# Reordering the start of layers 1 and 2: where the first products stand among the scores, and which transfers go ahead of the first spare rows

## The chip, the cores and the metric

The kernel runs on one core of a Trainium2 chip. Its engines are TensorE (PE, matrix products; the profile shows its weight loads apart as PEld), VectorE (DVE), ScalarE (ACT), GpSimd (POOL) and SyncE (SP), whose queue issues nearly all DMAs. Each engine works off its own list of instructions in order; semaphores hold an instruction back until its inputs are there. The metric is the device time of one execution in microseconds.

## The reference

The whole program is a convolution block followed by an attention block, on 32 images of 1024 channels and 14x14 positions. Only the first block matters here. It is made of three "lookup" layers: each splits its input channels into codebooks, scores every position against 16 centroids of each codebook, takes the softmax over the 16, and multiplies the result with a table of outputs:

```python
def _amm(patches, centroids, lut, inv_temp):
    B, D, H, W = patches.shape
    ncb, k, sub = centroids.shape
    v = patches.reshape(B, ncb, sub, H * W).transpose(0, 3, 1, 2)
    scores = 2.0 * einsum('blcs,cks->blck', v, centroids) - sum(centroids**2, -1)[None, None]
    attn = softmax(scores * inv_temp, axis=-1)
    out = einsum('blck,cko->blo', attn, lut)
    return out.transpose(0, 2, 1).reshape(B, -1, H, W)

out = _amm(x, c1_centroids, c1_lut, c1_invt)                       # layer 1: 1024 -> 256 channels
out = relu(_bn(out, bn1_g, bn1_b))
out = _amm(_extract3x3(out, 1), c2_centroids, c2_lut, c2_invt)     # layer 2: 3x3 patches of 256 -> 256
out = relu(_bn(out, bn2_g, bn2_b))
out = _amm(out, c3_centroids, c3_lut, c3_invt)                     # layer 3: 256 -> 1024
```

`x` here is the group-normalised input, and `_bn` takes its statistics over the whole batch, so a layer has to end before the next one can start.

## The kernel before, in words

Layers 1 and 2 are both run by one function, `units`. A unit is one pair of images (392 positions) times one eighth of the codebooks; there are 16 pairs, so 128 units in each layer, and unit `u` belongs to pair `u // 8` and table `u % 8`. A unit goes through these stations:

- `score(u)`: 4 score tiles by PE into PSUM (a pool `scores` of four buffers), then four exponentials by ACT (L576) into a tile `t`, one of six that are used in turn.
- `token_major`: a 32x32 block transpose on DVE (L588), and from unit 2 on a first halving addition on POOL (L591).
- `softmax`: sum, reciprocal and transpose back on DVE (L607, L609, L619), then POOL multiplies `t` by the reciprocals (L626). A unit with `u % 4 == 0` gives its first quarter to a tile `spare` (L621); for unit 0 POOL does the rest in three steps.
- `spare_rows` (L725, L728): DMAs on SP's queue that put rows of `spare` into every sixteenth row of `t`. Those rows are free because the 16 softmax weights of a codebook add to one: the last is left out, and the tables are corrected for it. So the first quarter of one unit in four is spread over the other quarters of the four, and that unit has 12 matmul records in place of 16.
- `lut(u)`: the products of `t` with the unit's table (L748) into the accumulators `po`, 12 or 16 matmul records.

The order in which these are written is the order on every engine (`tc.manual_schedule`). In step `i`, `units` writes `score(i + 4)` and its exponentials, the transpose of unit `i + 3`, the softmax of unit `i + 2` (of unit `i + 3` for units 0 and 1), then `side(i)`, a list of work by step, and last the products of one unit. The loop starts at `i = -4`. A small table at L784 says which products stand in the first steps:

```python
k = {-2: 0, -1: 1, 0: -1, 1: -1}.get(i, i) if ahead > 2 else i
```

So product 0 stands in step -2, product 1 in step -1, none in steps 0 and 1, and from step 2 on product `i`.

The eight tables of a layer lie in `weights`. `packed_lut` gives for each table the pieces of its preparation: `own` (piece 1, the load from HBM, L689 for layer 1 and four DMAs at L692 for layer 2), `less` (piece 2, a correction: two matmuls with `less_last`, L700, each evicted by ACT, L701), `keep` (piece 3, a DMA to a DRAM tile `tables`, L704) and `others` (piece 4, a DMA back from it into another table, L707).

In layer 1 the side work of the first steps also holds the group normalisation of the second image pair: statistics and means (L264, L274, L282), a power on POOL (L295), and the scaling of `x` on ACT (L825).

Layer 2 needs 3x3 patches. `store_pair(p, h)` normalises one half (128 of the 256 channels) of a pair into one of two `pads` (ACT, L990) and writes it by three DMAs (225 KB each, L1002) to two DRAM tiles `h1d`. `load_patches(u)` reads the patches of a unit from there by six DMAs (L1012) into one of four buffers. Units with table 0 to 3 use half 0, tables 4 to 7 half 1. `score2(u)` also loads the patches of unit `u + 3`. Before the first step, layer 2 writes this on SP's queue: the stores of half 0 of the first pair, patches 0 and 1 (a third of them on ACT's queue), `keep` of table 0, patches 2, `others` of table 0, patches 3, the stores of half 1, `others` of tables 1 to 3, and `own` of table 7. `own` of tables 0 to 6 is written late in layer 1. `side2` has the corrections of tables 4 to 7 in steps -3 to 0 and the stores of the later pairs, at a step given by the dictionary at L1065.

Of the kernel before, what the change touches and what calls it, by code (L numbers as in the profile page):

```python
# [149 lines left out]
def conv_preact_kernel(ctx: ExitStack, tc: tile.TileContext, a: dict, out: bass.AP):  # L150
# [3 lines left out]
    NP = B // 2  # L154
# [352 lines left out]
    def layers(exact, early=None):  # L507
# [38 lines left out]
        def tap_row(dy, dx):  # L546
            return 8 * dx + dy if dx < 2 else 3 + dy
# [25 lines left out]
        def exponentials(t, scs, bias):  # L573

            for j, sc in enumerate(scs):
                nc.scalar.activation(  # L576
                    t[:, j, : sc.shape[1]],
                    sc,
                    AF.Identity if exact else AF.Exp,
                    bias=bias[:, j : j + 1],  # L580
                )

        def token_major(pool, t, two=False, halve=False):


            tf = t.rearrange("p j n -> p (j n)")
            tt = pool.tile([P, tf.shape[1]], F32, tag="tt", name="tt", bufs=2 if two else 1)
            nc.vector.transpose(tt, tf)  # L588
            tv = tt.rearrange("p (m k) -> p m k", k=KC)
            if halve and not exact:  # L590
                nc.gpsimd.tensor_tensor(tv[:, :, :8], tv[:, :, :8], tv[:, :, 8:], ALU.add)  # L591
                tv = tv[:, :, :8]
            return tt, tv
# [123 lines left out]
        def spare_rows(ts, u):  # L717


            q = u % 4  # L720
            t, kept = ts[u % len(ts)], spares[u // 4 % 2]
            if exact and q == 0:
                nc.sync.dma_start(kept, t[:, 0, :N2])
            if q:
                nc.sync.dma_start(t[15::16], kept[q - 1 :: 4])  # L725
                return
            for j in range(1, 4):
                nc.sync.dma_start(t[15::16, j, :], kept[4 * j - 1 :: 16])  # L728
# [3 lines left out]
        def units(ahead, ts, pool, luts, score, bias, dst, stats, side, last, halve=False):  # L732

            n = 8 * NP
            po, late, tts = [], [], {}

            def lut(u):
                p, b = divmod(u, 8)  # L740
                if b == 0:
                    po[:] = [
                        ps_po.tile([P, 512], F32, tag="po", name="po")[:, :N2] for h in range(2)
                    ]
                j0 = 0 if b % 4 else 1
                order = [(h, j) for h in range(2) for j in range(j0, 4)]
                for h, j in order if b == 7 else sorted(order, key=lambda k: k[1]):
                    nc.tensor.matmul(  # L748
                        po[h],
                        luts[b][:, j, h * P : (h + 1) * P],  # L750
                        ts[u % len(ts)][:, j, :N2],
                        start=(b == 0 and j == j0),
                        stop=(b == 7 and j == 3),
                    )
                if b == 7:
                    for h in range(2):
                        o = dst[:, h, p * N2 : (p + 1) * N2]
                        nc.scalar.copy(o, po[h])
                        late.append((stats[:, h, p, :], o))

            for i in range(-ahead, n):
                u = i + ahead
                if u < n:
                    scs = score(u)
                    exponentials(ts[u % len(ts)], scs, bias[:, 4 * (u % 8) :][:, :4])
                u = i + ahead - 1
                if 0 <= u < n:
                    tts[u] = token_major(pool, ts[u % len(ts)], halve, halve and u >= DIRECT)
                if halve and u >= DIRECT:
                    u = u - 1 if u > DIRECT else n  # L770
                if 0 <= u < n:
                    softmax(
                        pool,
                        u,
                        ts[u % len(ts)],
                        *tts.pop(u),
                        spare=spares[u // 4 % 2] if u % 4 == 0 else None,
                        steps=(1, 1, 1) if u == 0 and not exact else None,
                    )
                    spare_rows(ts, u)  # L780
                while late:
                    nc.vector.bn_stats(*late.pop(0))
                side(i)
                k = {-2: 0, -1: 1, 0: -1, 1: -1}.get(i, i) if ahead > 2 else i  # L784
                if k >= 0:
                    lut(k)
            for h in range(2):
                nc.vector.bn_stats(*late.pop(0))
                last(h)
# [4 lines left out]
        with ExitStack() as s:  # L794
# [43 lines left out]
            def side(i):  # L838
                for f in todo.pop(i, []):
                    f()  # L840
# [10 lines left out]
            luts2 = [packed_lut(2, b) for b in range(8)]  # L851
# [120 lines left out]
        with ExitStack() as s:  # L972
# [4 lines left out]
            NPB = 4  # L977
# [10 lines left out]
            def store_pair(p, h, engines=(nc.sync,)):  # L988
                t = pads[h]
                nc.scalar.activation(  # L990
                    t.rearrange("p (i r c) -> p i r c", r=15, c=15)[:, :, :14, :14],
                    out1[:, h, p * N2 : (p + 1) * N2].rearrange(
                        "p (i r c) -> p i r c", r=14, c=14
                    ),
                    AF.Relu,
                    bias=bi1[:, h : h + 1],
                    scale=sc1[:, h : h + 1],
                )
                for x in range(3):
                    c0 = LEAD + 2 * p * IMG + 1 - x  # L1000
                    v = h1d[x // 2][h, :, :, c0 : c0 + 2 * IMG]
                    engines[x % len(engines)].dma_start(v[:, x::2] if x < 2 else v, t)  # L1002
# [3 lines left out]
            def load_patches(u, engines=(nc.sync,)):  # L1006
                p, b = divmod(u, 8)
                h, g = divmod(b, 4)
                for n, (src, rows) in enumerate(zip(h1d, (8, 16))):
                    for dy in range(3):  # L1010
                        c0 = LEAD + 2 * p * IMG + 15 * (dy - 1)
                        engines[dy % len(engines)].dma_start(  # L1012
                            pbuf[u % NPB][tap_row(dy, 2 * n) :: rows, :, :SPAN],
                            src[h, 4 * g : 4 * g + 4, :, c0 : c0 + SPAN].rearrange(
                                "q r n -> r q n"
                            ),
                        )
# [10 lines left out]
            load_patches(2)  # L1028
            luts2[0][4]()
            load_patches(3)  # L1030
            store_pair(0, 1)
            for b in range(1, 4):
                luts2[b][4]()
            luts2[7][1]()
            w9, bias2 = parts[2]

            def score2(u):
                if 0 < u and u + NPB - 1 < 8 * NP:
                    load_patches(u + NPB - 1)
                scs = [scores(N2) for j in range(4)]  # L1040
                for c in range(4):
                    for j, sc in enumerate(scs):
                        r = slice(32 * j, 32 * j + 27)
                        v = pbuf[u % NPB][r, c].rearrange("p (i r c) -> p i r c", r=15, c=15)
                        nc.tensor.matmul(
                            sc[32 * c : 32 * c + 32],
                            w9[r, u % 8 * 4 + c],
                            v[:, :, :14, :14],
                            start=True,
                            stop=True,  # L1050
                        )
                return scs

            ahead = 1 if exact else 4

            def side2(i):

                for b in range(4, 8):
                    if i == max(b - 7, -ahead):
                        luts2[b][2]()  # L1060
                    if i == max(b - 4, 0):
                        luts2[b][4]()
                if i == max(-2, -ahead):
                    luts2[4][3]()
                p = {1: 1}.get(i + ahead, (i + ahead + 9) / 8)  # L1065
                if p in range(1, NP):
                    for h in range(2):
                        store_pair(int(p), h)
                if i == 60:
                    bias3, biases = score_biases(ps_tr, big, st, 3, raw[3], P, 2, mask8, 4)  # L1070
                    parts[3] = score_matrices(big, 3, "", raw[3], mask8), bias3
                    parts["biases3"] = biases
                if i == 64:
                    parts["biases3"]()
                next_lut3(i - 8 * (NP - 1) - 1)
# [1213 lines left out]
```

## Time and profile before

| | us |
|---|---|
| median of three runs | 3391.9 |
| lowest and highest of them | 3390.8, 3393.84 |
| the profiled execution's own time | 3393.07 |
| its span, first to last instruction | 3390.4 |
| PE busy | 3303.7 (97%) |
| DVE busy | 2871.6 (85%) |
| POOL busy | 2528.6 (75%) |
| ACT busy | 1790.1 (53%) |
| mean granted clock of TensorE | 0.994 |

Layer 1 runs from about 20 to 834 us of the span, layer 2 from there to about 1648 us, each with a start of some 50 us in which its pipeline fills.

How to read the profile's lines. A timeline line is: start, length, engine, line of the kernel, operation, output <- inputs, shapes, count of instructions that were merged into the line, and in brackets how long the engine was idle before it and what ended that idle time. PE's matmul records are halves: one fp32 matmul shows as two. A line of a table of stretches is: the stretch, its length, busy time and instruction count of PE, PEld, DVE, ACT and POOL, the granted clock (1.00 is full speed), the mean share of the DMA engines, and GB/s. "SPq" lines are the issue of DMAs by SP, not their transfer.

### The profile page before, as it was taken

The page shows a single profiled execution, that of the slowest core. Times are in us where ns is not written, and L with a number is a line of the kernel's source. Part 1 is how long each engine was busy: PE and PEld are TensorE (multiplying, and loading weights), DVE is VectorE, ACT ScalarE, POOL GpSimd, SP SyncE. Part 2 cuts the span into 40 slices and gives each one's busy share as a digit, 9 for nine tenths or more (in the row PEclk, how much of TensorE's full clock was granted, in tenths as well). Part 3 has the DMA queues.
Part 4 walks back from the last instruction along what each step waited for, and adds up shares of the span by engine and source line. Part 5 has one row for each costly group of instructions (what it writes and reads, how often), then busy time and mean ns, then how long its engine had stood idle before and what let it go on. Part 6 is the DMA issues. An engine that isn't in the chain of part 4 may idle for free. (4 is left out here: it accounts for less than half of the span.)

```text
span 3390.4 us, 61032 instructions
## 1 busy us (share of the span) xinstructions
PE 3303.7 (97%) x22287; PEld 2015.7 (59%) x22287; DVE 2871.6 (85%) x4174; ACT 1790.1 (53%) x4419; POOL 2528.6 (75%) x1562
## 2 busy tenths in 40 slices
PE   7999999999899999999999999999999999999998
PEld 4555555554344444454478888876666666666665
DVE  7999999997788898888666666655899999989996
ACT  4555555554444444444311111108888888888885
POOL 4999999997688888888432222216998889898887
PEclk9999999999999999999999999999999999999999
DMA  3111110102444344443231111113223333233221
GB/s 119 47 32 45 46 47 28 46 27 75 136 126 122 111 122 124 117 117 109 63 80 49 49 49 50 49 47 123 67 85 88 89 93 93 79 99 96 73 87 39
DMA packets 242251, 266.31 MB, mean 79 GB/s; under 512 B 32812, under 2 KB 239700, under 8 KB 241944
## 3 DMA queue, kind: packets, MB, share of 16 engines
q1 hardware_dynamic: 241128, 261.85, 26.3%
q8 instruction: 179, 2.93, 0.4%
q14 instruction: 128, 1.05, 0.1%
q10 hardware_dynamic: 816, 0.48, 0.0%
HBM read 171.01 MB, written 75.58 MB: 73 GB/s over the span
## 5 line engine op out<-in xcount | busy, mean ns | idle before, releaser
L626 POOL TENSOR_TENSOR t<-t,r 128x1568 f32<-128x1568 f32 (+5 forms) x292 | 962.1, 3296 | 528.9 <-issue 222.3
L748 PE MATMUL po<-t,lut 128*128 128x392 f32 x3840 | 1334.5, 500 | 13.3 <-DMA t<-spare 7.4
L748 PEld LDWEIGHTS po<-t,lut 128*128 128x128 f32 x3840 | 711.6, 190 | 614.8 <-issue 86.9
L1796 PE MATMUL mm<-y,lut 128*128 128x392 f32 x2048 | 713.5, 494 | 5.5 <-ACT vt L1861 4.1
L588 DVE STREAM_TRANSPOSE tt<-t 128x1568 f32<-128x1568 f32 (+1 forms) x284 | 517.5, 1822 | 158.7 <-ACT t L576 154.5
L576 ACT ACTIVATE t<-sc,cbias 128x392 f32<-128x392 f32 (+1 forms) x624 | 322.3, 597 | 562.8 <-PE sc L910 188.3
L2020 DVE SCALAR_TENSOR_TENSOR pa<-y,lepe_w,pa 128x406 f32<-128x406 f32 x900 | 534.5, 638 | 22.2 <-PE pa L2002 19.9
L619 DVE STREAM_TRANSPOSE r<-rc 128x1568 f32<-128x1568 f32 (+1 forms) x284 | 520.9, 1834 | 11.6 <-POOL t L626 1.2
L1796 PEld LDWEIGHTS mm<-y,lut 128*128 128x128 f32 x2048 | 370.0, 188 | 249.0 <-ACT vt L1861 5.0
L591 POOL TENSOR_TENSOR tt<-tt 128x784 f32<-128x784 f32 x252 | 463.4, 1839 | 29.9 <-DVE tt L588 29.8
L576 ACT ACTIVATE t<-sc,room 128x392 f32<-128x392 f32 x512 | 259.0, 588 | 392.0 <-issue 163.3
L1378 PE MATMUL po<-t,lut 128*128 128x224 f32 (+2 forms) x1352 | 313.3, 414 | 0.0
L607 DVE TENSOR_REDUCE sm<-tt 128x98 f32<-128x784 f32 (+2 forms) x284 | 297.1, 1046 | 1.2 <-POOL tt L591 0.8
L1378 PEld LDWEIGHTS po<-t,lut 128*128 128x128 f32 (+1 forms) x1352 | 233.4, 189 | 62.9 <-issue 60.6
L609 DVE RECIPROCAL rc<-sm 128x98 f32<-128x98 f32 (+1 forms) x284 | 220.2, 775 | 9.8
L630 ACT ACTIVATE sm<-sm 128x98 f32<-128x98 f32 (+1 forms) x284 | 85.1, 300 | 160.4 <-DVE rc L609 160.3
L1649 ACT ACTIVATE w<-x,tb,gn_a 128x196 f32<-128x196 f32 x248 | 128.3, 518 | 39.9 <-POOL y L1531 28.3
L1982 POOL TENSOR_TENSOR qr<-qr,zb 128x784 f32<-128x784 f32 x64 | 118.0, 1854 | 29.0 <-DMA zb<-zd 26.1
L1808 ACT ACTIVATE e<-e 128x392 f32<-128x392 f32 x256 | 134.4, 525 | 1.4
L825 ACT ACTIVATE x<-x,gn_b,gn_a 128x196 f32<-128x196 f32 x256 | 127.6, 557 | 5.1 <-POOL gn_b L296 3.4
L1762 ACT ACTIVATE y<-x,gb,ga 128x196 f32<-128x196 f32 x256 | 122.8, 542 | 13.6 <-POOL gb L1725 13.4
L1391 DVE TENSOR_TENSOR o<-po,o 128x224 f32<-128x224 f32 (+1 forms) x156 | 81.6, 543 | 56.7 <-PE po L1378 51.9
(215 smaller groups left out, 4520.4 us busy)
## 6 DMA issues: line engine op xcount, KB each, us to landing
patch<-h1d SPq DMA_DIRECT2D x382, 108.5 KB
x<-in_x_dram SPq DMA_DIRECT2D x32, 784.0 KB
o3d<-o SPq DMA_DIRECT2D x56, 448.0 KB
x<-in_x_dram SPq DMA_DIRECT2D x64, 392.0 KB
out_dram<-x SPq DMA_DIRECT2D x64, 392.0 KB
o<-o3d SPq DMA_DIRECT2D x62, 392.0 KB
h1d<-pad SPq DMA_DIRECT2D x96, 225.0 KB
patch<-h1d SPq DMA_DIRECT2D x382, 54.2 KB
```

The costliest lines, as they stand in the source:

```text
L576: nc.scalar.activation(t[:, j, : sc.shape[1]], sc, AF.Identity if exact else AF.Exp, bias=bias[:, j : j + 1],)
L588: nc.vector.transpose(tt, tf)
L591: nc.gpsimd.tensor_tensor(tv[:, :, :8], tv[:, :, :8], tv[:, :, 8:], ALU.add)
L607: nc.vector.tensor_reduce(sm, tv, AX.X, ALU.add)
L609: nc.vector.reciprocal(rc, sm)
L619: nc.vector.transpose(r, bc(rc, 2, KC))
L626: nc.gpsimd.tensor_tensor(v[:, c], v[:, c], r[:, c], ALU.mult)
L748: nc.tensor.matmul(po[h], luts[b][:, j, h * P : (h + 1) * P], ts[u % len(ts)][:, j, :N2], start=(b == 0 and j == j0), stop=(b == 7 and j = ...
L1378: nc.tensor.matmul(dst, w, x, start=start, stop=stop)
L1796: nc.tensor.matmul(pv(), w[kt][:, m0 : m0 + P], ywin(p, first + kt), start=(kt == 0), stop=(kt == 3),)
L1808: nc.scalar.activation(e(), e(), AF.Exp, scale=-1.0)
L2020: nc.vector.scalar_tensor_tensor(acc, neighbours(p, c, offset(k)), lw[:, c, k : k + 1], acc, ALU.mult, ALU.add,)
```

## The change

In both layers the products of the first steps stand elsewhere: product 0 stays in step -2; product 1 moves from step -1 to step 0, behind the scores of unit 4; product 2 from step 2 to step 1, behind the scores of unit 5; product 3 stays in step 3; steps -1 and 2 have none.

In layer 2 the stores of half 1, `others` of table 1 and patches 4 are put into a function that is called in step -3, behind the spare rows of unit 0; patches 4 were written at the start of step -3 before. `others` of tables 2 and 3 and `own` of table 7 are called in step -2. The stores of the second pair go from step -3 to step 0. The branch `exact` (a slower repeat of the layers that runs only if a softmax sum overflows) keeps its order.

```diff
-                k = {-2: 0, -1: 1, 0: -1, 1: -1}.get(i, i) if ahead > 2 else i
+                k = {-2: 0, -1: -1, 0: 1, 1: 2, 2: -1}.get(i, i) if ahead > 2 else i
...
             load_patches(3)
-            store_pair(0, 1)
-            for b in range(1, 4):
-                luts2[b][4]()
-            luts2[7][1]()
+
+            def second_half():
+                store_pair(0, 1)
+                luts2[1][4]()
+                if not exact:
+                    load_patches(NPB)
+
+            def more_tables():
+                luts2[2][4]()
+                luts2[3][4]()
+                luts2[7][1]()
+
+            if exact:
+                second_half()
+                more_tables()
             w9, bias2 = parts[2]
 
             def score2(u):
-                if 0 < u and u + NPB - 1 < 8 * NP:
+                if u > (0 if exact else 1) and u + NPB - 1 < 8 * NP:
                     load_patches(u + NPB - 1)
...
             def side2(i):
 
+                if i == 1 - ahead and not exact:
+                    second_half()
+                if i == 2 - ahead and not exact:
+                    more_tables()
                 for b in range(4, 8):
...
-                p = {1: 1}.get(i + ahead, (i + ahead + 9) / 8)
+                p = {4: 1}.get(i + ahead, (i + ahead + 9) / 8)
```

## The prediction

> **What bounds the kernel now.** I read the busy row of the page first, then the list of what TensorE (PE) waits for, then the timelines of the two stretches in which layers 1 and 2 fill their pipelines, and last the granted clock there.
>
> ```profile
> PE 3303.7 (97%) x22287; PEld 2015.7 (59%) x22287; DVE 2871.6 (85%) x4174; ACT 1790.1 (53%) x4419; POOL 2528.6 (75%) x1562
> ```
>
> PE is busy for 97% of the span, and in layer 1 between 80 and 830 us the list of its waits is empty. One unit costs PE 5.53 us of products and 0.94 of scores, and the starts of its scores are spaced just so. A microsecond of PE time saved in a fill is therefore kept to the end, if PE is again the engine that lags once the pipeline is full. The fill of layer 1, PE first, then DVE and POOL:
>
> ```profile
> 39.73 0.94 PE L910 MATMUL sc<-x,cw 32*128 32x392 f32 x8
> 41.33 1.98 PE L700 MATMUL sc<-lut,less_last 128*128 128x512 f32 x4 [0.66 <-ACT t L576]
> 45.73 7.20 PE L748 MATMUL po<-t,lut 128*128 128x392 f32 x16 [2.42 <-POOL tt L591]
> 52.86 0.94 PE L910 MATMUL sc<-x,cw 32*128 32x392 f32 x8
> ...
> 64.64 1.40 PE L910 MATMUL sc<-x,cw 32*128 32x392 f32 x4 [1.41 <-ACT lut L701]
> 65.97 7.23 PE L748 MATMUL po<-t,lut 128*128 128x392 f32 x16
> ...
> 58.55 0.20 DVE L282 TENSOR_TENSOR gd<-gst,gn_ps 128x32 f32<-128x32 f32 x1 [9.66 <-PE gn_ps L274]
> ...
> 61.26 1.83 POOL L591 TENSOR_TENSOR tt<-tt 128x784 f32<-128x784 f32 x1 [8.72 <-DVE tt L588]
> ```
>
> The product of unit 1 (45.73) waits for its rows, and unit 4's scores (52.86) stand behind it, so DVE, POOL and ACT all run dry for about 9 us. Both products of 16 records take 7.2 us where 5.53 is usual. The clock says why, and the same in layer 2 (the last number before the DMA share is the clock):
>
> ```profile
> 47.00:48.00 1.00, 1.00 (x3) 0.64 (x2) 0.97 (x2) 0.00 (x0) 0.19 (x1) 0.50 0.41 54
> 68.00:69.00 1.00, 1.00 (x3) 0.37 (x3) 0.96 (x2) 0.00 (x0) 1.00 (x2) 0.50 0.00 0
> 867.00:868.00 1.00, 1.00 (x3) 0.54 (x2) 0.00 (x0) 0.00 (x0) 0.00 (x0) 0.50 1.04 375
> ```
>
> The fill of layer 2, with the queue of SP and one wait of ACT:
>
> ```profile
> 853.66 1.36 SPq L1002 DMA_DIRECT2D h1d<-pad x3
> 855.06 1.95 SPq L707 DMA_DIRECT2D lut<-tables x3
> 857.11 1.81 SPq L692 DMA_DIRECT2D lut<-in_lut_dram x4
> 859.02 3.73 SPq L1012 DMA_DIRECT2D patch<-h1d x6
> 862.86 1.98 SPq L728 DMA_DIRECT2D t<-spare x3
> ...
> 857.60 0.71 ACT L990 ACTIVATE pad<-out,bi,sc 128x392 f32<-128x392 f32 x1 [3.78 <-DMA h1d<-pad]
> ...
> 858.84 3.68 PE L700 MATMUL sc<-lut,less_last 128*128 128x512 f32 x4 [4.65 <-ACT t L576]
> 864.95 5.88 PE L748 MATMUL po<-t,lut 128*128 128x392 f32 x12 [2.44 <-issue]
> ...
> 915.25 5.50 PE L748 MATMUL po<-t,lut 128*128 128x392 f32 x16 [2.68 <-DMA t<-spare]
> ```
>
> Unit 0's spare rows (862.86) are ready on POOL from 855.9 (three steps of 1.0 us from 854.87) and stand behind 14 other transfers; the product of unit 0 follows 2.1 us after them. PE last waits at 915.25, then runs without a gap.
>
> **Layer 1: only the order of products changes.** Up to product 0 (ends 39.8) nothing moves. I place each step at the later of "engine free" and "input there", with the durations above; ACT takes 2.0 us for four exponentials and 1.05 for two evictions of a corrected table, DVE 5.3 for a unit, POOL 1.83 and 3.5, spare rows land 2.1 us after issue.
> - Scores 4 now go ahead of product 1: 43.3 to 45.0 (two PSUM slots come from ACT's copies at 44.0 and 44.55). The corrections of tables 5 and 6 (1.9 us each) run to 49.1, the two mean matmuls to 49.6.
> - Product 1: 49.6 to 55.1. Its rows are there since 45.7, so its 2.42 us wait is gone.
> - Scores 5 to 56.0, table 7 and the second means to 58.8 (paced by the exponentials), product 2 to 64.3 (rows landed 54.7).
> - Scores 6 to 65.2; scores 7 need its exponentials to leave PSUM, to 66.9; product 3 starts 66.9 against 74.00: 7.1 us ahead.
> - What is late next: scores 8 need the second pair's normalisation. Its factors come from POOL after unit 4 (2.92 us power, 72.3 now against 77.7), ACT ends the first block at 73.35, PE idles 1.0 us. Product 4: 74.3 against 80.33, so **6.0 us** remain; products 5 and 6 come out at 5.9.
>
> The clock is in that sum. The row: each long wait is followed by a stretch of about 3.4 us at 0.50 (46.6 to 50.0, 67.1 to 70.5), on a grid of 3.4 us. The Trainium skill, "TensorE: Matmul & The Clock Gate", section "Part 1: The HAM clock gate", has the rule: a free-running window of about 3.4 us, in which too little PE work halves the clock of what follows. The trace agrees and shows the level: windows with 1.0 us (43.2 to 46.65) and about 1.6 us of real matmul time were followed by 0.50; one with about 2.3 (882.9 to 886.3) was not. In the new order each window of the fill holds at least 2.2, so I count no half clock: product 1 and 2 save 1.7 us each, 3.4 of the 6.0. The rule read strictly (the phase of the grid is free) would allow one bad window: 4.3 instead of 6.0.
>
> **Layer 2: order, and the queue of SP.** The queue stands free at 853.55 (after patches 3). It is one queue, issued in order, so I walk it with its own durations:
> - Spare rows of unit 0 at 855.9, 856.9, 857.8, as POOL finishes its three steps. SP waits 2.3 us here, as the cost of the move.
> - Then the stores of pad h=1 (1.36), table 1 (0.65): 860.5. Patches 4 read what the stores wrote; before, two other transfers covered that, now the wait stands open on SP. Row: stores issued to 855.02, pad free at 857.6, so 2.5 us. [...] I take the row: 862.3.
> - Patches 4 and 5 to 869.9, spare rows 1, tables 2 and 3 to 871.8, the load of table 7 (1.81) to 873.7 (before: 858.9), patches 6 and 7 to 881.8 (before 880.84), spare rows 2 at 882.4, pad pair 1 (2.84) to 885.9, a second open wait of about 1 us, patches 8, spare rows 3 at 891.5.
>
> PE beside it:
> - ACT's pad of h=1 (0.72) now precedes the copies of table 4: scores 2 end 855.1 against 854.2. The 3.78 us wait for the pad is gone from ACT: exponentials 2 end 857.4 against 860.2, table 5 ends 858.3.
> - Product 0: 858.4 to 864.3, again at half clock (PE is idle before it), against 864.95 to 870.83. **6.5 us ahead.**
> - Scores 3, table 6, scores 4 (patches 4 landed 868.5) to 869.6.
> - **What is late next:** the correction of table 7 stands on PE ahead of product 1, and its load is issued to 873.7. No row shows this landing; bounds are 2.1 us (spare rows) and 5 (twice the store); I take 2.5, the row of the stores, nearest in size: 876.2. PE idles 6.6 us, works at half clock to 879.6: table 7 to 879.8, product 1 to 885.3. Before, the same work (scores 4, table 7, product 1) was done at 883.3. **The 6.5 us are spent, 2.0 are lost.**
> - Products 2 (886.2 to 891.7) and 3 (895.6 to 901.1, before to 899.9), 4 to 906.2, 5 to 912.6. Now the units are 9 us earlier on DVE, so the late POOL no longer holds product 6: spare rows 6 land 913.6, product 6 ends 919.1 against 920.75. **1.65 us ahead**; from there PE runs full in both. Bounds: 2 us behind (table 7 lands at 880) to 4 ahead.
>
> Sum: 5.9 + 1.6 = 7.5 us, from the profiled execution (3393.07 us; its span 3390.4 lies 2.7 below). The median of the runs is 1.2 us under that execution: 3391.9 - 7.5 = **3384.4**.
>
> **The rivals.**
> 1. *Layer 2 gives back, layer 1 is clipped by the clock* (0.24): table 7 lands 3 to 5 us later than I took and one half-clock window falls in layer 1. 4.3 - 2 = 2.3 saved, down to nothing: 3386 to 3392. For it: SP has 28 us of transfers in a row and two open waits. Against: 1.6 us of slack at product 6.
> 2. *More than I count* (0.20): DVE and POOL, 9 us ahead in layer 2, and table 7 landing at once (875) also spare the half-clock window: 6 + 4 and up to 1.7 more: 3380 to 3382.
> 3. *DVE sets the pace of layer 1* (no case of its own): it is 96% busy there and gains only 4.8 us (unit 8's transpose 79.6 against 84.38). Against: PE trails a unit's softmax by two units, so the 1.1 us are made up.
> 4. *Slower* (0.11): SP's queue stands. One mechanism: patches 4 wait on the completed stores, and everything behind (patches 5, spare rows 1, table 7) waits too. At 883.7 for table 7's landing the whole gain is gone (7.5 us later than taken); at 890.5 the kernel is 0.2% slower, 3398.7 and more. The stores' landing would have to take 10 us where 2.5 were seen.
>
> **How the numbers follow.** 0.2% is 6.8 us, about what a measurement of this kernel can tell from no change; the border to "faster" is 3385.1. The main case has 0.45 and spans 3381.5 to 3388; about two thirds of it, 0.31, lie under the border, 0.14 above. Faster: 0.31 + 0.20 (rival 2) = 0.51. Within 0.2%: 0.14 + 0.24 (rival 1) = 0.38. Slower: 0.11 (rival 4). The range runs from 3378.5 (a little past rival 2) to 3392.5 (the end of rival 1) and leaves out rival 4 and small tails, under 2 in 10.
>
> **What would show it.** Layer 1: scores 4 before product 1, no idle of 9 us on DVE and POOL, products 1 and 2 near 5.5 us, product 6 near 86.3. Layer 2: product 0 starting at 858 on that clock (6 us less for layer 1's gain), no wait of ACT for the pad, then one PE idle of 6 to 7 us before the correction of table 7, and no wait before product 6. Wrong if table 7's correction doesn't wait (then the gain is near 10), if SP stands over 5 us before patches 4, or if DVE, not PE, is what products wait for between 100 and 800 us.

## The result, and the profile after

The changed kernel takes 3369.53 us (median of 4 runs, 3369.28 to 3371.3), the kernel before 3391.59 beside it: ratio 0.9935, 95% interval 0.9918 to 0.9952. That is 22 us less, where 7.5 were forecast and the range ended at 13 less. The experiments below show that these 22 us are two things: the edit of the diff is worth 5.4 us, and about 17 belong to layer 4, which the diff does not touch.

The first lines of the profile's page after:

```profile
span 3367.6 us, 61031 instructions
PE 3297.9 (98%) x22287; PEld 2011.5 (60%) x22287; DVE 2868.9 (85%) x4174; ACT 1788.6 (53%) x4419; POOL 2528.4 (75%) x1562
```

PE has almost the same work (3303.7 before) in a span 22.8 us shorter. Where that lies is read from PE's timeline: the same five points of the program, found in both profiles, divide the span into stages.

| stage (ends at the start of ...) | before | after | saved |
|---|---|---|---|
| start, to the end of layer 1's product 0 | 39.8 | 37.8 | 2.0 |
| layer 1 (first correction of a table for layer 2, L700) | 794.3 | 788.7 | 5.6 |
| fill of layer 2 (scores of its unit 11) | 86.6 | 86.9 | -0.3 |
| rest of layer 2 (first scores of layer 3) | 730.8 | 731.9 | -1.1 |
| layer 3 (first product of layer 4, L1796 before, L1811 after) | 659.1 | 659.0 | 0.1 |
| layer 4 | 1079.8 | 1063.4 | 16.5 |

The 1.1 us lost in the rest of layer 2 are not the edit's: the changed order of layers 1 and 2 takes 730.0 and 730.7 us there in two later profiles (`new_dve`, `new_dve_again`).

The fill of layer 1 after the change, PE's timeline and a line of DVE:

```profile
41.22 2.28 PE L910 MATMUL sc<-x,cw 32*128 32x392 f32 x8
43.43 3.70 PE L700 MATMUL sc<-lut,less_last 128*128 128x512 f32 x8
46.97 0.51 PE L274 MATMUL gn_ps<-gst,gavg 128*128 128x16 f32 x4
47.33 5.51 PE L748 MATMUL po<-t,lut 128*128 128x392 f32 x16
52.78 0.94 PE L910 MATMUL sc<-x,cw 32*128 32x392 f32 x8
...
56.56 5.51 PE L748 MATMUL po<-t,lut 128*128 128x392 f32 x16
...
65.95 5.54 PE L748 MATMUL po<-t,lut 128*128 128x392 f32 x16
...
47.52 0.20 DVE L282 TENSOR_TENSOR gd<-gst,gn_ps 128x32 f32<-128x32 f32 x1 [0.65 <-PE gn_ps L274]
```

Products 1, 2 and 3 (47.33, 56.56, 65.95) wait for nothing and take 5.5 us each; before, products 1 and 2 took 7.2. Scores 4 (41.22) stand ahead of product 1, so DVE is idle for 0.65 us before L282, where it was idle for 9.66. A new wait of 3.16 us, for the next means at 56.75, costs it part of that.

The fill of layer 2, PE, then DVE, then SP's queue:

```profile
850.38 4.19 PE L748 MATMUL po<-t,lut 128*128 128x392 f32 x12
...
859.98 0.95 PE L1056 MATMUL sc<-patch,room 27*32 27x392 f32 x32 [1.77 <-DMA patch<-h1d]
867.65 3.75 PE L700 MATMUL sc<-lut,less_last 128*128 128x512 f32 x4 [6.72 <-DMA lut<-in_lut_dram]
871.19 6.44 PE L748 MATMUL po<-t,lut 128*128 128x392 f32 x16
877.57 0.94 PE L1056 MATMUL sc<-patch,room 27*32 27x392 f32 x32
...
907.90 5.50 PE L748 MATMUL po<-t,lut 128*128 128x392 f32 x16 [2.16 <-DMA t<-spare]
...
880.70 1.81 DVE L588 STREAM_TRANSPOSE tt<-t 128x1568 f32<-128x1568 f32 x1 [12.29 <-ACT t L576]
...
848.56 2.52 SPq L728 DMA_DIRECT2D t<-spare  x3
851.18 1.35 SPq L1002 DMA_DIRECT2D h1d<-pad  x3
852.58 0.62 SPq L707 DMA_DIRECT2D lut<-tables  x1
853.99 7.55 SPq L1012 DMA_DIRECT2D patch<-h1d  x12
...
863.53 1.87 SPq L692 DMA_DIRECT2D lut<-in_lut_dram  x4
...
884.30 3.72 SPq L1012 DMA_DIRECT2D patch<-h1d  x6
889.85 1.85 SPq L728 DMA_DIRECT2D t<-spare  x3
```

On a clock set to layer 2's first correction (826.48 here, 834.11 before, so 7.63 apart) product 0 starts 6.9 us earlier than before. All of it is given back at 867.65, where PE stands 6.72 us for table 7, whose load is now issued behind patches 4 and 5. Product 1 and scores 5 (877.57) stand behind that correction in PE's order, so DVE is idle for 12.29 us until it gets unit 5 (880.70).

### The profile page after: what moved, and what is told of

It is laid out like the page before. It is cut to its first block, busy times and chain, and to the rows that moved or that the text cites. A ratio compares the mean times of both kernels' runs of the same rounds, so it can differ in the third digit from the quotient of the medians.

```text
span 3367.6 us, 61031 instructions
## 1 busy us (share of the span) xinstructions
PE 3297.9 (98%) x22287; PEld 2011.5 (60%) x22287; DVE 2868.9 (85%) x4174; ACT 1788.6 (53%) x4419; POOL 2528.4 (75%) x1562
## 5 line engine op out<-in xcount | busy, mean ns | idle before, releaser
L1811 PE MATMUL mm<-y,lut 128*128 128x392 f32 x2048 | 714.6, 494 | 2.0 <-DVE k L1827 2.0
L2035 DVE SCALAR_TENSOR_TENSOR pa<-y,lepe_w,pa 128x406 f32<-128x406 f32 x900 | 536.4, 637 | 19.3 <-PE pa L2017 17.0
L1811 PEld LDWEIGHTS mm<-y,lut 128*128 128x128 f32 x2048 | 369.4, 188 | 243.7 <-issue 6.3
```

Of the source, the lines that this page charges most:

```text
L1811: nc.tensor.matmul(pv(), w[kt][:, m0 : m0 + P], ywin(p, first + kt), start=(kt == 0), stop=(kt == 3),)
L2035: nc.vector.scalar_tensor_tensor(acc, neighbours(p, c, offset(k)), lw[:, c, k : k + 1], acc, ALU.mult, ALU.add,)
```

## The experiments

### The order of layer 4 held fixed

Layer 4 is not written by hand. `Plan.write` (L83) plays its pieces through and issues them in the order that it finds, and at each moment it asks the engines one after the other, in the order of a set of names:

```python
engines = {p[0] for p in self.pieces}     # "PE", "DVE", "ACT", "POOL", "SP"
...
for e in engines:
```

Python walks a set of strings in another order in each process, so this order is drawn anew when the program is built. It decides ties: pieces of DVE and POOL marked `port=True` exclude each other, and when both may start at once, the engine that is asked first takes the place. The 120 orders of the five names make only two programs: one whenever POOL stands ahead of DVE, one whenever DVE stands ahead. `Plan.write` returns the end of its own clock, which needs no chip: 1102.7 us for the first, 1084.8 for the second, 17.9 apart. From layer 4's first product on, POOL's 846 instructions stand in the trace before in exactly the order of the kernels with POOL first below, and in the trace after in exactly the order of those with DVE first. So the two kernels compared above differ in layer 4 as well, and four kernels separate this from the edit. Each has one line changed, in the file before ("old") or in the file after ("new"):

```diff
-        engines = {p[0] for p in self.pieces}
+        engines = ["POOL", "DVE", "PE", "ACT", "SP"]     # or "DVE", "POOL", ...
```

> The order before in layers 1 and 2; in Plan.write the engines are walked as a fixed list with POOL ahead of DVE, in place of a set of names. Theory A (layer 4's planned order differs between the two programs measured, because the set of names is walked in another order in each build, and that is 15 to 16 us of the 22): this is the program of the profile before, 3390 to 3394 us. Theory B (the edit gives all 22 us, the last 16 because layer 4 starts 6 us earlier in its clock windows and its transfers): also 3390 to 3394.

> The order before in layers 1 and 2; DVE ahead of POOL in the list that Plan.write walks. Theory A: 3375 to 3377 us (3391.6 less the 15 to 16 us by which layer 4 is shorter in the profile after). Theory B: as with POOL first, 3390 to 3394, since the edit is not there.

> The changed order in layers 1 and 2; POOL ahead of DVE in the list. Theory A: 3384 to 3387 us (3391.6 less what the profiles show at the start of layer 3, 6.3). Theory B: 3369 to 3371.

> The changed order in layers 1 and 2; DVE ahead of POOL. Theory A: this is the program of the profile after, 3369 to 3371 us, 6 to 7 under the old order with the same list. Theory B: 3369 to 3371 too, but 22 under the old order with the same list.

Measured, all on one chip, beside 3394.1 for the kernel before:

| | POOL first | DVE first |
|---|---|---|
| old order in layers 1 and 2 | 3394.61; ratio 1.0001 (0.9992 to 1.0009) | 3374.91; 0.9947 (0.9933 to 0.9960) |
| new order in layers 1 and 2 | 3389.28; 0.9986 (0.9979 to 0.9993) | 3369.52; 0.9930 (0.9916 to 0.9943) |

Theory A holds and B falls, which wanted 3369 to 3371 for the new order with POOL first. A's own figures were met less closely: 3389.28 lies 2.3 us above its range there, and 3374.91 just below the other. Down a column, the edit is worth 5.3 and 5.4 us; along a row, the tie is worth 19.7 and 19.8. Together that is 25 us and not the 22 of the first comparison, since the kernel before took 3394.1 here and 3391.59 there; so what the tie costs is known to some 3 us. The two are independent: layer 4 takes 1079.8 to 1082.2 us in the three profiles with POOL first and 1062.3 to 1063.4 in the three with DVE first, whichever order stands in layers 1 and 2. "Before" is the POOL-first program, "after" the DVE-first one.

What the tie costs is seen in the busy times of layer 4 by stretch (columns: length, then busy time and count of PE, PEld, DVE, ACT, POOL, clock, DMA). The old order with POOL first:

```profile
2311.60:2600.00 288.40, 283.85 (x2535) 182.01 (x2536) 234.44 (x500) 248.55 (x623) 251.04 (x230) 1.00 0.26 75
2600.00:2900.00 300.00, 295.50 (x2972) 191.88 (x2970) 287.11 (x610) 253.62 (x620) 263.21 (x238) 1.00 0.31 90
2900.00:3200.00 300.00, 292.84 (x2710) 189.77 (x2710) 282.91 (x607) 251.73 (x623) 263.96 (x240) 1.00 0.31 88
...
3300.00:3391.90 91.90, 78.05 (x768) 48.98 (x757) 63.20 (x102) 53.36 (x131) 74.14 (x66) 0.96 0.14 43
```

and with DVE first:

```profile
2307.80:2600.00 292.20, 290.26 (x2561) 186.25 (x2561) 244.51 (x518) 256.63 (x642) 258.22 (x235) 1.00 0.27 77
2600.00:2900.00 300.00, 297.88 (x3013) 194.49 (x3012) 289.13 (x616) 253.10 (x625) 263.06 (x242) 1.00 0.33 93
2900.00:3200.00 300.00, 296.36 (x2871) 192.50 (x2873) 287.47 (x611) 254.11 (x627) 268.66 (x245) 1.00 0.31 89
...
3300.00:3370.10 70.10, 62.59 (x664) 39.46 (x662) 42.04 (x75) 42.33 (x101) 57.49 (x49) 0.97 0.15 47
```

PE's idle time is length less busy. With POOL first it is 4.6, 4.5, 7.2 and, at the end, 13.9 us; with DVE first 1.9, 2.1, 3.6 and 7.5. With the quiet 100 us from 3200 on (0.6 and 0.2) that is 30.7 against 15.4: 15 of the 18 us by which these two layers 4 differ; PE's busy time, 2.8 us longer, is the rest. Of the 15 us, about 9 lie in small waits along the whole layer, and 6 behind 3300. The end shows how. The denominators of the last pair (PE L1946), their use on POOL (L1982) and the last additions on DVE, POOL first:

```profile
3364.50 1.53 PE L1946 MATMUL mm<-q,kmm 128*32 128x196 f32 x32
3370.41 7.24 POOL L1982 TENSOR_TENSOR qr<-qr,zb 128x784 f32<-128x784 f32 x4 [2.88 <-ACT zb L1988]
3379.42 5.57 DVE L2020 SCALAR_TENSOR_TENSOR mm<-y,lepe_w,mm 128x406 f32<-128x406 f32 x10 [0.77 <-PE mm L2002]
```

and DVE first:

```profile
3325.43 1.53 PE L1946 MATMUL mm<-q,kmm 128*32 128x196 f32 x32
3335.00 5.48 POOL L1982 TENSOR_TENSOR qr<-qr,zb 128x784 f32<-128x784 f32 x3 [0.23 <-ACT zb L1988]
```

With POOL first the denominators come 27 us before the end, and a chain of PE, DVE, PE, ACT, POOL, PE and DVE follows, and from 3370.6 on PE has nothing to do but this chain's own work. With DVE first they come 45 us before the end, and other products run beside the chain. That the tie decides this is shown; which single tie along the way moved the chain to the end was not tried.

### Which part of the edit works

From here on every kernel has the DVE-first list, so layer 4 is the same (1061.9 to 1063.0 us in all profiles). First, layer 1's order alone:

```diff
-                k = {-2: 0, -1: 1, 0: -1, 1: -1}.get(i, i) if ahead > 2 else i
+                first = {-2: 0, -1: -1, 0: 1, 1: 2, 2: -1} if stats is stats1 else {-2: 0, -1: 1, 0: -1, 1: -1}
+                k = first.get(i, i) if ahead > 2 else i
```

> DVE-first list throughout; the new order of products in layer 1 only, layer 2 wholly as before. If layer 1's order carries the edit: layer 1 from the end of its product 0 to the first correction of layer 2 takes 788.7 us (794.3 before), layer 2 from there to its twelfth scores 86 to 86.6, and the time is 3369 to 3371 us, as with the whole edit. If layer 2's part gives what the prediction counted (1.65): 1 to 2 us more than the whole edit.

3367.67 us (3365.08 to 3371.22), the ratio to the kernel before 0.9925 (0.9909 to 0.9942). Layer 1 takes 788.7 us, the fill of layer 2 87.3. The ratio is that of the whole edit with this list (0.9930) within the scatter of both: layer 1's order carries it, and layer 2's part is worth nothing that these runs can tell.

Second, the whole edit, but the products of layer 2 in the old order (the same `first` line in the file after):

> DVE-first list; layer 1 new, layer 2 with the new order of transfers and the old order of products (product 1 ahead of scores 4 and of the correction of table 7). If the stand before table 7's correction is what eats layer 2's gain: product 1 fills it (863.8 to 870 on the clock of the profile after), product 3 ends 3 us earlier, and the twelfth scores come 1 to 3 us earlier (84 to 86 us after the first correction). If the moved products were what layer 2 needed: 88 to 92.

3367.98 us (3365.02 to 3368.67), fill of layer 2 85.7. So the moved products of layer 2 are no help: product 1 ahead of table 7's correction uses the stand. But it is not free either; it now waits 5.72 us. The profile names nothing for this wait, but product 1's own spare rows were issued at 861.54, 2.3 us before it starts:

```profile
863.83 8.33 PE L748 MATMUL po<-t,lut 128*128 128x392 f32 x16 [5.72 <-issue]
```

Third, the load of table 7 goes into the gap in which SP waits for POOL's first spare rows:

```diff
             load_patches(3)
+            if not exact:
+                luts2[7][1]()
...
                 luts2[3][4]()
-                luts2[7][1]()
+                if exact:
+                    luts2[7][1]()
```

> The whole edit, DVE-first list, with one more move: the load of table 7 goes right behind patches 3 on SP's queue, into the 2.3 us in which SP waits for POOL's first spare rows. Theory: the 6.7 us wait before its correction is gone; then spare rows 2, 3 and 6 in SP's queue are late next, 1 to 2 us earlier than now: twelfth scores 84 to 85.5 us after the first correction (86.5 now), the time 1 to 2 us under the whole edit. Rival (the wait was the whole loss): 79 to 80.

3367.17 us (3366.01 to 3368.55), fill 85.4. The 6.7 us are gone, and product 2 (877.04) stands instead:

```profile
863.33 1.98 PE L700 MATMUL sc<-lut,less_last 128*128 128x512 f32 x4 [0.75 <-ACT t L576]
865.83 5.50 PE L748 MATMUL po<-t,lut 128*128 128x392 f32 x16 [0.52 <-DMA t<-spare]
...
877.04 8.00 PE L748 MATMUL po<-t,lut 128*128 128x392 f32 x16 [4.83 <-DMA t<-spare]
```

Taking one wait away gained 1.1 us of the fill (86.5 in `new_dve`) out of 6.7, since the next in the same queue was 5 us behind it. So, fourth, with table 7 early, the patches of three units later are issued behind each step's spare rows:

```diff
-                if u > (0 if exact else 1) and u + NPB - 1 < 8 * NP:
+                if exact and u > 0 and u + NPB - 1 < 8 * NP:
                     load_patches(u + NPB - 1)
...
                 if i == 2 - ahead and not exact:
                     more_tables()
+                u = i + ahead + NPB - 1
+                if i > 1 - ahead and not exact and u < 8 * NP:
+                    load_patches(u)
```

> As the kernel with table 7 early, and in every step of layer 2 the patches for three units later are issued behind that step's spare rows instead of ahead of them. Theory (SP's order is what holds PE): no product waits for spare rows any more, the twelfth scores come 76 to 80 us after the first correction, the time is 7 to 9 us under the whole edit, 3360 to 3363. Rival (POOL and DVE hold the products): 84 to 86, as with table 7 early alone.

3363.12 us (3359.89 to 3365.8), fill 78.9. PE in the same places, products 1, 2 and 6:

```profile
862.58 5.43 PE L748 MATMUL po<-t,lut 128*128 128x392 f32 x16
...
870.32 5.51 PE L748 MATMUL po<-t,lut 128*128 128x392 f32 x16 [1.44 <-issue]
...
899.48 5.50 PE L748 MATMUL po<-t,lut 128*128 128x392 f32 x16 [0.19 <-DMA t<-spare]
```

With table 7 early, the order of SP's queue is what holds PE in this fill, not POOL or DVE. The fill is as short as the theory had it. That no product would wait for spare rows was not met in full (1.44 us are left at product 2, whose rows were issued 2.3 us before it), and the time fell a little short.

Last, this kernel and the whole edit with the same list, once more beside each other:

> The whole edit with the DVE-first list once more, beside the next kernel on one chip: 3367 to 3371 us.

> Table 7 early and the patches behind the spare rows, once more: if layer 2's fill is really 7.6 us shorter (78.9 against 86.5 in the profiles), 5 to 8 us under the kernel beside it, 3360 to 3365.

3368.69 us (3365.9 to 3370.37) and 3361.84 (3361.3 to 3365.77): 6.9 us apart, with fills of 87.0 and 78.7. Against the kernel before (3392.23) the last has the ratio 0.9912 (0.9899 to 0.9926), the shortest time of this study. Of its 30 us, some 20 are the list in `Plan.write`.

## Why the prediction was wrong

**The step that failed** is in the sum: it let everything from layer 3 on stand as it was ("a microsecond of PE time saved in a fill is therefore kept to the end"). Layer 3 did stand (659.1 and 659.0 us). Layer 4 did not: it is 16.5 us shorter, since the program is another one there, and nothing in the diff says so. The quoted sentence itself held; what failed is that the forecast put layer 4's own change at nothing, without asking how its order comes about. The diff of two sources was taken for the difference of two programs. No rival had this case. The profile of before could not show it, as it is one program of two; line 90 of the kernel could.

**The edit itself** was forecast at 7.5 us and measured at 5.3 and 5.4. By its steps:
- Layer 1: forecast 5.9, in the profiles 5.6. The order of events came as walked: on a clock set to the end of product 0, product 1 starts at 49.35 (49.6 forecast), product 4 at 74.3 (74.3). No half clock falls in this fill in any of the profiles with the new order (1.00 between 27 and 100 us), as forecast. That 5.6 comes so near to 5.9 is in part luck: the old order with DVE first shows no half clock there either in its one profile, its layer 1 takes 792.2, and against this the edit saves 3.5 us. The 3.4 us for the clock were thus an upper end; how many half-clock windows the old order meets varies from run to run.
- The level that was read for the clock (about 1.6 us of matmul time too little, 2.3 enough) does not come out of the later profiles: in the old order with POOL first, the 3.4 us from 912.4 hold 1.45 us of PE work, all of it products, and the clock stays at 1.00 behind them. What level decides is open.
- Product 0 of layer 2: forecast at 858.4 and at half clock, seen (7.63 added) at 858.0 and at full clock, 4.19 us.
- Table 7: forecast a stand of 6.6 us, seen 6.72. Its load landed 2.25 us after the end of its issue; 2.5 were taken, from the stores.
- The end of the fill: forecast 1.65 us ahead, seen 0.3 behind. The step that failed here is "Now the units are 9 us earlier on DVE". That came for units 3 and 4, whose transposes start 8.6 and 12 us earlier, and ended with unit 5, whose scores stand behind table 7's correction and product 1: its transpose starts at 888.3 on the clock of before, where it started at 888.04 before the change. The softmax of unit 4 stands behind it on DVE, so its spare rows were not ready: SP, which was on time until then (spare rows 3 issued to 891.2, 891.5 forecast), stood 1.8 us before spare rows 4 (889.85). With that stand in the queue, spare rows 6 came about 2 us later than forecast: 2.16 us of wait at product 6, where 0.1 was counted.
- Rival 1's range does not follow from its sum: 2.3 us saved, down to nothing, is 3389.6 to 3391.9, not from 3386 on.
- Rival 3 (DVE sets layer 1's pace) and rival 4 (SP's queue makes it slower) did not come; the stand on the stores in SP's queue before patches 4 is under 1 us (852.58 + 0.62 to 853.99).
- The first 2.0 us of the stage table are none of the edit's: product 0 of layer 1 ends between 37.3 and 37.8 in the profiles whose clock is 1.00 from 15 to 27 us, and between 39.0 and 39.9 in those where it is 0.86. All three profiles with the old order of layer 1 fell among the latter, and four of the nine with the new; up to there the two programs are the same.

## What to carry to other kernels

Before a time is compared, compare the order of instructions of the two programs engine by engine, also where the diff is silent: an order that a planner finds may hang on something that is no part of the source, and a tie in it was worth more than three times the edit here. Give such a planner a fixed order for its ties, and compare the times that it plays through for each, since that is a free choice: here its own clock had the 18 us. And in a queue that is worked off in order, a wait is seldom alone: write down when each of the next few entries is needed, for taking away the first stand of 6.7 us shortened the fill by 1.1, and putting the whole queue in the order of need shortened it by about 8.

## What was not expected of the hardware

The half clock is a matter of phase. In each profile its windows stand on a grid of 3.4 us, which lies elsewhere against the kernel's first instruction each time: the half-clock windows before product 0 of layer 1 begin at 17.0, 18.1 and 19.3 us in the three profiles of the old order. So the same instructions before that product's end come out up to 2.5 us apart (37.3 and 39.9), and the old layer 1 took 792.2 or 794.3 us. In the fill of layer 2 after the change the clock is 0.53 from 835 to 845 and 0.54 from 862 to 873 us, and product 1 takes 6.44 us in place of 5.5. But this is no mark of the change: over that fill the mean clock is 0.94, 0.90 and 0.86 in the three profiles of the old order, and 0.88, 0.86, 0.88 and 0.86 in the four of the whole edit. A forecast finer than some 2 us of such a fill needs several executions of both kernels.
